# Four banks and a second pass for a fused layer's downsampling, with its constant operators made earlier

## The chip, the cores and the metric

The kernel runs on one core of one Trainium2 chip. The metric is the device time of one execution in microseconds; smaller is better. The program is written in Python on top of a planner: the program names the tiles, the instructions and the pools, and the planner places the instructions of each engine in an order of its own and adds the waits.

## The reference, cut to what matters

Four layers are computed on eight images of 512 channels by 32 x 32 pixels, in f32. Layer 0 is a group norm, a multi-head attention with an iterated tanh step, and a projection. Layer 1 is one attention over all 1024 pixels. Layer 3 is a bottleneck of mixed experts. The change concerns layer 2: every channel of every image is upsampled by two with a 12-tap filter, passed through a leaky ReLU, and downsampled by two with the same kind of filter.

```
out = input + bias
out = sep_upfirdn(out, up_filter * 2, up=2)
out = leaky_relu(out, 0.2) * sqrt(2)
out = sep_upfirdn(out, down_filter, down=2)
```

The filters are inputs, so the matrices that the kernel uses for them must be made on the chip.

## The kernel before, in words

An outer loop runs over the images. For each it does layer 0, layer 1 and layer 2, and stores the result; layer 3 follows for all images. The eight PSUM banks are in three pools: `ps_sc` has two tiles of two banks each, and `ps_tp` and `ps_mm` have two single banks each. SBUF tiles of the tag `tmp` (1024 columns) share six slots, those of the tag `half` (512 columns) two.

Layer 0 multiplies by blocks in Winograd's manner: `product` (L387 to L422) computes seven products named P1, C11, U2, U3, C22, C21 and C12 into three pairs of banks A, X and Y, and the callback `made` evicts each. For v the callback `positions` does it on VectorE (DVE). In the first image, the weights' sums are made on GpSimd (POOL) by `weight_sums`, one key after the other: q, k, v, inl, proj and v1. Each has a raw tile of tag `tmp` or of its own.

Layer 1 ends in `weighted_rows`, whose matmuls (L905) leave pixel rows in `y`. They are written to a padded image in DRAM and read back, with their halo, by `Halo.load`. In the first image `layer2_constants` follows. It builds the operators `up_op`, `up_left_op`, `dn_op`, `up63_op` and `dn63_op` in scratch columns of one `tmp` tile named `setup`: two loads of taps and ten iotas on POOL, then several hundred short instructions on DVE that compare an index with each tap's number and add.

Layer 2 has eight tiles of rows, t = 0 to 7. `upsample(t)` does four matmuls by column block c (each is two records in the trace), into banks that turn through `ps_sc` and `ps_tp`. The helper `leak` then makes the leaky ReLU in two steps, `leak` on ScalarE (ACT, L954) and `up` on DVE (L955). `downsample(first, last, ts_)` collects the rows of two or three tiles t. For each chunk of 128 channels, cc = 0 to 3, it opens a bank of `ps_mm` and adds one matmul per block (t, c) and per half of 64 channels (L995), then evicts the bank to `z`. The calls are

```
upsample 0 1 2   downsample(0, 13, (0, 1, 2))
upsample 3 4     downsample(9, 21, (3, 4))
upsample 5 6 7   downsample(17, 31, (5, 6, 7))
```

with a last small strip (`up_63`, L1031; `dn63_op`, L1003) before and in the third downsampling. The eviction is an ACT copy after the first call (L1009), two DVE instructions after the second (L1011, L1012), and a DVE addition, an ACT copy and a DVE reduction after the third.

The order of an engine's instructions is the planner's. It starts from its own times for each instruction and, among those that are ready, serves first what is written first. Exceptions are regions that the program marks with `tc.manual_schedule(engines=...)`, in which the named engines keep the written order among the region's instructions; layer 0's attention is one. SyncE's queue (SP) issues the loads of x, the weights and the halos; POOL's issues the taps and the stores of the weights' sums; ACT's issues most of the writes of `y`.

A second copy of the whole program with shifted exponents (`shifted`) follows in a conditional block. It runs only when sums overflow, which they do not with these inputs.

Of the kernel before, what the change touches and what calls it, by code (L numbers as in the profile page):

```python
# [12 lines left out]
ALU = mybir.AluOpType  # L13
AX = mybir.AxisListType
# [3 lines left out]
P = 128  # L18
B, C, H, W = 8, 512, 32, 32
S = H * W  # L20
CC = C // P
SC = S // P
HALF = 512
NH = 8
HD = C // NH
# [28 lines left out]
def tile_sequence(ctx: ExitStack, tc: tile.TileContext, a: dict, out: bass.AP, shifted: bool):  # L54
# [12 lines left out]
    def big_tile(name, shape):  # L67
        return big.tile(shape, F32, tag="big", name=name)

    def bank(pool=None, name="mm"):  # L70
        pool = pool or ps_mm
        return pool.tile([P, HALF], F32, tag="bank", name=name)

    def tmp(name, n=HALF):
        if n == HALF:
            return work.tile([P, n], F32, tag="half", name=name, bufs=2)
        return work.tile([P, n], F32, tag="tmp", name=name, bufs=6)
# [260 lines left out]
    def weight(key, b):  # L338
        if not b:
            return weight_sums(key, *weight_quarters(key, tmp(f"raw_{key}", S)))  # L340
        t = wpool.tile([P, len(PARTS), 2, QR], F32, tag="w", name=f"w_{key}_{b}", bufs=3)
        nc.sync.dma_start(t, stored[key])
        return t
# [225 lines left out]
    def layer0(b, x, norm, w):  # L569
# [9 lines left out]
        w["inl"] = weight("inl", b)  # L579
        all_of(product(f"k_{b}", w["k"], h, t, channels(f"k_{b}", k, qkv_b[:, CC : 2 * CC])))  # L580
        w["proj"] = weight("proj", b)
        early = small.tile([P, 1], F32, tag="early", bufs=1, name=f"early_{b}")
        tc.keep_in_program_order(nc.scalar.activation(early, eps, AF.Exp))
        all_of(product(f"v_{b}", w["v"], h, t, positions(f"v_{b}", v, v_row), rows=True))
# [19 lines left out]
        def scores(t):  # L604
            g, jc = divmod(t, SC)
            oc, sh = groups[g]
            pair = ps_sc.tile([P, S], F32, tag="scores", name=f"scores_{b}_{t}")
            ps = [pair[:, ts(r, HALF)] for r in range(2)]
            for r in range(2):
                for c in range(2):  # L610
                    nc.tensor.matmul(  # L611
                        ps[r][rows[c]],
                        k[rows[r], oc, jc * P + c * HD : jc * P + c * HD + HD],
                        q[rows[r], oc, ts(sh, HALF)],
                        start=True, stop=(shifts is None),
                    )
            if shifts is not None:
                for r in range(2):
                    nc.tensor.matmul(
                        ps[r], ones[HD * r : HD * r + 1, :],  # L620
                        shifts[HD * r : HD * r + 1, oc, ts(sh, HALF)],
                        start=False, stop=True, skip_group_check=True,
                    )
            e = tmp(f"e_{b}_{t}", S)
            nc.scalar.activation(e, pair, AF.Exp, scale=HD ** -0.5)  # L625
            exps[t] = e
            if jc == 1:
                accs[g] = sums(f"acc_{b}_{g}")
                nc.vector.tensor_add(accs[g], exps[t - 1], e)  # L629
            elif 1 < jc < SC - 1:  # L630
                nc.vector.tensor_add(accs[g], accs[g], e)  # L631
            elif jc == SC - 1:
                nc.vector.scalar_tensor_tensor(
                    accs[g], accs[g], 1.0, e, ALU.mult, ALU.add,
                    accum_out=seen_sums[:, b, g : g + 1],
                )
# [84 lines left out]
    def layer1(b, x, w, midway):  # L721
# [109 lines left out]
                midway()  # L831

        weighted_rows(b, eT, v, inv, y, written)
        if b == 0:
            layer2_constants()
        for t in range(3, NT):
            halo.load(t)
        halo.load_last()
# [108 lines left out]
    def layer2(b, halo, freed=lambda t: None):  # L947


        up = []  # L950

        def leak(dst, ps, name):
            t = tmp(f"leak_{name}")[0 : dst.shape[0], :]
            nc.scalar.mul(t, ps, 0.2 * SQRT2)  # L954
            nc.vector.scalar_tensor_tensor(dst, ps, SQRT2, t, ALU.mult, ALU.max)  # L955

        def upsample(t):
            if t % 2 == 0:
                two = big_tile(f"up_{b}_{t // 2}", [P, 8, C])
                up.extend(two[:, 4 * i : 4 * i + 4, :] for i in range(2))  # L960
            for c in (0, 2):

                n = 2 * t + c // 2
                if n % 3 == 2:
                    ps = [bank(ps_tp, name=f"up_{b}_{t}_{c + i}") for i in range(2)]
                else:
                    pair = ps_sc.tile([P, S], F32, tag="scores", name=f"up_{b}_{t}_{c}")
                    ps = [pair[:, ts(i, HALF)] for i in range(2)]
                for i in range(2):
                    _, n, op = halo.columns(c + i)  # L970
                    nc.tensor.matmul(  # L971
                        ps[i], op[0 : IR * n, :], halo.tile(t)[0 : IR * n, c + i, :],
                        start=True, stop=True,
                    )
                for i in range(2):
                    leak(up[t][:, c + i, :], ps[i], f"{b}_{t}_{c + i}")

        halves = [slice(0, HD), slice(HD, P)]  # L980

        def downsample(first, last, ts_):
            for cc in range(CC):
                zr = z[:, cc, :].rearrange("p (h w) -> p h w", w=W)
                ps = bank(name=f"dn_{b}_{cc}_{first}")
                rows = ps.rearrange("p (h w) -> p h w", w=W)
                blocks = [(t, c) for t in ts_ for c in range(4)]
                for i, (t, c) in enumerate(blocks):
                    r0, r1 = max(4 * t - 3, 0), min(4 * t + 5, H - 1)
                    c0, c1 = max(8 * c - 3, 0), min(8 * c + 10, W - 1)  # L990

                    k = P - UC if t == 0 else P
                    op = dn_op[0:k].rearrange("p (r c) -> p r c", c=OC)
                    for s, part in enumerate(halves):
                        nc.tensor.matmul(  # L995
                            rows[part, r0 - first : r1 + 1 - first, c0 : c1 + 1],
                            up[t][0:k, c, ts(2 * cc + s, HD)],
                            op[:, r0 - 4 * t + 3 : r1 + 4 - 4 * t, c0 - 8 * c + 3 : c1 + 4 - 8 * c],
                            start=(i == 0), stop=(last < H - 1 and i == len(blocks) - 1),
                            skip_group_check=True,  # L1000
                        )
                for s, part in enumerate(halves if last == H - 1 else ()):
                    nc.tensor.matmul(  # L1003
                        ps[part, (29 - first) * W : (32 - first) * W],
                        up63[:, ts(2 * cc + s, HD)], dn63_op,
                        start=False, stop=True, skip_group_check=True,
                    )
                if first == 0:
                    nc.scalar.copy(zr[:, 0:14, :], rows[:, 0:14, :])  # L1009
                elif first == 9:  # L1010
                    nc.vector.tensor_add(zr[:, 9:14, :], rows[:, 0:5, :], zr[:, 9:14, :])  # L1011
                    nc.vector.tensor_copy(zr[:, 14:22, :], rows[:, 5:13, :])  # L1012
                else:
                    nc.vector.tensor_add(zr[:, 17:22, :], rows[:, 0:5, :], zr[:, 17:22, :])
                    nc.scalar.copy(zr[:, 22:32, :], rows[:, 5:15, :])
                    nc.vector.tensor_reduce(pooled[:, cc, b : b + 1], z[:, cc, :], AX.X, ALU.add)
                    if b + 1 < B:
                        nc.sync.dma_start(spilled[b][ts(cc, P), :], z[:, cc, :])
            freed(ts_[-1])

        for t in range(3):
            upsample(t)
        z = big_tile(f"z_{b}", [P, CC, S])
        downsample(0, 13, (0, 1, 2))
        for t in (3, 4):
            upsample(t)
        downsample(9, 21, (3, 4))
        for t in (5, 6, 7):
            upsample(t)
        ps = bank(ps_tp, name=f"up_{b}_63")  # L1030
        nc.tensor.matmul(ps, up63_op[0 : 3 * W, :], halo.last, start=True, stop=True)  # L1031
        up63 = tmp(f"up63_{b}")
        leak(up63, ps, f"{b}_63")
        freed(6)
        downsample(17, 31, (5, 6, 7))
        return z

    with tc.tile_pool(name=f"weights_{run}", bufs=1) as wpool:
# [136 lines left out]
    def freed(t):  # L1175
        if t == 4:
            load_experts("w2_0", 3 * P)
            z3[0] = load_z(0)
        elif t == 6:
            for ky in (1, 2):  # L1180
                load_experts(f"w2_{ky}", 3 * P)
        elif t == 7:
            load_experts("w3", C)
# [119 lines left out]
```

## Time and profile before

| what | value |
|---|---|
| median of 3 runs | 3828.78 us (3828.47 to 3829.96) |
| the profiled execution | 3826.37 us, span 3824.6 us |
| TensorE (PE) busy | 3764.8 us, 98% |
| VectorE (DVE) busy | 2572.6 us, 67% |
| ScalarE (ACT) busy | 1202.9 us, 31% |
| GpSimd (POOL) busy | 100.3 us, 3% |
| dn matmuls, L995 | 4096 records, 210.5 us busy |
| up matmuls, L971 | 512 records in eight images |

In the profile, PE is the matmuls and PEld the weight loads that overlap them. Each f32 matmul is two records. A line of the timeline gives start, length, engine, line, operation, written and read tiles, shape and count, and in brackets the idle time of the engine ahead of it with what ended it.

### The profile page before, as it was taken

Reading aid. Unit: us, or ns where it says so; the run is one execution under the profiler, and the core shown is the slowest. Engines: PE = TensorE matmul, PEld = TensorE weight load, DVE = VectorE, ACT = ScalarE, POOL = GpSimd, SP = SyncE. Lnnn points to the kernel's source line nnn. Section 1 sums busy time; section 2 is a strip of 40 time slices with the busy share of each in tenths; the row PEclk is TensorE's granted clock in tenths of the full one; section 3 lists DMA queues with packets and bytes.
Section 4 is the critical chain, followed back from the end, with each engine's and each line's share of the span. In section 5 each row is a group of like instructions: output and inputs, shape, how many; then the busy total and the mean of one; then the engine's idle time right before and its main releaser. Section 6 shows DMA issues by size and latency. Waiting matters only on the chain.

```text
span 3824.6 us, 50438 instructions
## 1 busy us (share of the span) xinstructions
PE 3764.8 (98%) x20838; PEld 1996.0 (52%) x20838; DVE 2572.6 (67%) x3887; ACT 1202.9 (31%) x1707; POOL 100.3 (3%) x118
## 2 busy tenths in 40 slices
PE   8999999999999999999999999999999999999999
PEld 4346653475435753466534754357534754347543
DVE  5877948664686648775586647765487656866885
ACT  0631226212442116312252124422162123521333
POOL 5000000000000000000000000000000000001000
PEclk9999999999999999999999999999999999999999
DMA  5002310123101310023101220023201131003432
GB/s 199 24 1 86 115 63 1 42 76 106 39 1 61 121 70 11 1 85 119 58 1 61 84 92 27 1 80 102 80 1 42 52 129 41 1 1 124 161 145 98
DMA packets 85841, 248.67 MB, mean 65 GB/s; under 512 B 10480, under 2 KB 33024, under 8 KB 78816
## 3 DMA queue, kind: packets, MB, share of 16 engines
q1 hardware_dynamic: 69712, 220.23, 16.2%
q10 hardware_dynamic: 13824, 12.59, 1.0%
q0 software_dynamic: 2064, 12.51, 0.9%
q8 instruction: 166, 2.72, 0.3%
q14 instruction: 75, 0.61, 0.1%
HBM read 185.40 MB, written 59.90 MB: 64 GB/s over the span
## 4 chain that ended last, share of the span: by engine, by line
PE 93%; DVE 4%; ACT 1%; DMA 1%; issue 0%; SPq 0%; ACTq 0%; DVEq 0%
PE scores L611 12%; PE av L647 12%; PE inl_X L417 6%; PE dn L995 5%; PE v_X L417 4%; PE inl_A L417 4%; PE inl_Y L417 4%; PE up L971 4%; PE av_X L905 3%; PE c L1209 3%; PE v_Y L417 3%; PE av_A L905 3%; PE av_Y L905 2%; PE v_A L417 2%; PE proj_X L417 2%; PE q_X L417 2%
## 5 line engine op out<-in xcount | busy, mean ns | idle before, releaser
L625 ACT ACTIVATE e<-scores 128x1024 f32<-128x1024 f32 x512 | 523.2, 1024 | 673.5 <-PE scores L611 624.8
L611 PE MATMUL scores<-q,k 64*64 64x512 f32 x4096 | 535.8, 593 | 3.6 <-DVE v L498 3.6
L647 PE MATMUL av<-e,v 64*64 64x512 f32 x4096 | 531.0, 589 | 0.0
L631 DVE TENSOR_TENSOR acc<-acc,e 128x1024 f32<-128x1024 f32 x320 | 389.5, 1217 | 38.5 <-ACT e L625 36.5
L611 PEld LDWEIGHTS scores<-q,k 64*64 64x64 f32 x4096 | 153.8, 133 | 297.6 <-issue 208.5
L647 PEld LDWEIGHTS av<-e,v 64*64 64x64 f32 x4096 | 161.3, 133 | 278.2 <-issue 275.2
L417 PE MATMUL inl_X<-T_hf,w_inl 128*128 128x512 f32 x576 | 262.9, 592 | 0.0
L955 DVE SCALAR_TENSOR_TENSOR up<-up,leak 128x512 f32<-128x512 f32 x264 | 173.5, 688 | 115.3 <-ACT leak L954 110.0
L954 ACT ACTIVATE leak<-up 128x512 f32<-128x512 f32 x264 | 149.5, 596 | 249.5 <-DVE up L955 127.7
L668 DVE RECIPROCAL inv<-av 128x256 f32<-128x256 f32 x128 | 223.0, 1747 | 0.0
L995 PEld LDWEIGHTS dn<-dn_op,up 128*64 128x64 f32 (+1 forms) x4096 | 193.2, 136 | 56.5 <-issue 28.8
L995 PE MATMUL dn<-dn_op,up 128*64 128x126 f32 (+5 forms) x4096 | 210.5, 255 | 8.8 <-DVE up L955 7.9
L971 PE MATMUL up<-halo,up_op 126*128 126x512 f32 (+1 forms) x384 | 183.7, 611 | 0.8 <-DVE up L955 0.6
L417 PEld LDWEIGHTS inl_X<-T_hf,w_inl 128*128 128x128 f32 x576 | 108.7, 190 | 138.6 <-issue 105.8
L417 PE MATMUL inl_A<-hf,w_inl 128*128 128x512 f32 x384 | 172.2, 594 | 0.0
L511 ACT ACTIVATE inl_U<-inl_U,inl_b 128x512 f32<-128x512 f32 x96 | 66.7, 718 | 307.6 <-DVE inl_U L526 307.6
L629 DVE TENSOR_TENSOR acc<-e,e 128x1024 f32<-128x1024 f32 x64 | 78.8, 1232 | 112.0 <-ACT e L625 112.0
L522 DVE TENSOR_TENSOR inl_U<-inl_X,inl_P 128x512 f32<-128x512 f32 x96 | 61.9, 687 | 121.7 <-PE inl_X L417 118.9
L1209 PE MATMUL c<-rim,mixed 128*128 128x512 f32 x288 | 124.9, 592 | 0.0
L417 PEld LDWEIGHTS inl_A<-hf,w_inl 128*128 128x128 f32 x384 | 72.2, 190 | 94.6 <-issue 90.4
L905 PE MATMUL av_X<-v,eT 128*128 128x256 f32 x512 | 118.8, 380 | 1.8 <-DVE av_W L884 1.0
L905 PE MATMUL av_A<-v,eT 128*128 128x256 f32 x512 | 119.1, 381 | 0.0
(304 smaller groups left out, 5561.1 us busy)
## 6 DMA issues: line engine op xcount, KB each, us to landing
halo<-ypad_u SPq DMA_DIRECT2D x128, 252.0 KB
halo<-ypad_u SPq DMA_DIRECT2D x128, 198.0 KB
w_v<-stored_u_v SPq DMA_DIRECT2D x14, 1792.0 KB
x<-in_x_dram SPq DMA_DIRECT2D x32, 512.0 KB
spill_u<-z SPq DMA_DIRECT2D x28, 512.0 KB
z<-spill_u SPq DMA_DIRECT2D x28, 512.0 KB
out_dram<-z SPq DMA_DIRECT2D x28, 512.0 KB
w_q<-stored_u_q SPq DMA_DIRECT2D x7, 1792.0 KB
```

Of the source, the lines that this page charges most:

```text
L417: nc.tensor.matmul(dst, lhs, rhs, start=(opens and s == 0 and cc == 0), stop=(cc == 1 and s == rows), skip_group_check=True,)
L611: nc.tensor.matmul(ps[r][rows[c]], k[rows[r], oc, jc * P + c * HD : jc * P + c * HD + HD], q[rows[r], oc, ts(sh, HALF)], start=True, stop= ...
L625: nc.scalar.activation(e, pair, AF.Exp, scale=HD ** -0.5)
L631: nc.vector.tensor_add(accs[g], accs[g], e)
L647: nc.tensor.matmul(avs[g][r][rows[c]], v[rows[r], jc, ts(2 * oc + c, HD)], e[rows[r], ts(c, HALF)], start=(jc == 0), stop=(jc == SC - 1),)
L668: nc.vector.reciprocal(copies[g][:, at], totals[g][:, at])
L905: nc.tensor.matmul(ps[:, ts(s, QR)], left[:, j, at : at + P], right[:, j, :], start=(what in ("P1", "U2", "W") and s == 0 and j == 0), sto ...
L954: nc.scalar.mul(t, ps, 0.2 * SQRT2)
L955: nc.vector.scalar_tensor_tensor(dst, ps, SQRT2, t, ALU.mult, ALU.max)
L971: nc.tensor.matmul(ps[i], op[0 : IR * n, :], halo.tile(t)[0 : IR * n, c + i, :], start=True, stop=True,)
L995: nc.tensor.matmul(rows[part, r0 - first : r1 + 1 - first, c0 : c1 + 1], up[t][0:k, c, ts(2 * cc + s, HD)], op[:, r0 - 4 * t + 3 : r1 + 4 ...
L1209: nc.tensor.matmul(banks[g].rearrange("p (h w) -> p h w", w=W), wt[:, at : at + P], h1[:, ky + 16 * g : ky + 16 * g + 16, kx : kx + W], st ...
```

## The change

It has four parts. `layer2_constants()` is called in layer 0 of the first image, after the product for k and the request of the projection's weights, and no longer at the end of layer 1. The downsampling opens four banks at once, two of `ps_mm` and two of `ps_tp`; a first pass adds all rows of blocks but the last to each, and a second pass adds the last row and evicts. The upsampling's turn of banks is moved by one (`n % 3 == 1`). The PE instructions of layer 2 stand in a region of fixed order. Besides, a bias matmul of the shifted program is cut in two halves.

```
@@ layer0
         w["proj"] = weight("proj", b)
+        if b == 0:
+            layer2_constants()
         early = small.tile([P, 1], F32, tag="early", bufs=1, name=f"early_{b}")
...
@@ layer1
         weighted_rows(b, eT, v, inv, y, written)
-        if b == 0:
-            layer2_constants()
...
@@ layer2
-                if n % 3 == 2:
+                if n % 3 == 1:
                     ps = [bank(ps_tp, name=f"up_{b}_{t}_{c + i}") for i in range(2)]
...
+        def down_block(rows, cc, first, last, t, c, opens, closes):
...
         def downsample(first, last, ts_):
-            for cc in range(CC):
-                ps = bank(name=f"dn_{b}_{cc}_{first}")
-                blocks = [(t, c) for t in ts_ for c in range(4)]
-                for i, (t, c) in enumerate(blocks):
...
+            ends = last == H - 1
+            banks = [bank((ps_mm, ps_tp)[cc // 2], f"dn_{b}_{cc}_{first}") for cc in range(CC)]
+            for late in range(2):
+                for cc in range(CC):
+                    rows = banks[cc].rearrange("p (h w) -> p h w", w=W)
+                    for t in ts_[-1:] if late else ts_[:-1]:
+                        for c in range(4):
+                            down_block(
+                                rows, cc, first, last, t, c, t == ts_[0] and c == 0,
+                                late == 1 and c == 3 and not ends,
+                            )
+                    if late:
+                        evicted(cc, banks[cc], rows, first, ends)
             freed(ts_[-1])
...
+        with tc.manual_schedule(engines={mybir.EngineType.PE}):
+            for t in range(3):
+                upsample(t)
+            z = big_tile(f"z_{b}", [P, CC, S])
+            downsample(0, 13, (0, 1, 2))
...
```

`down_block` is the matmul pair of one block as before, and `evicted` the strip's matmuls and the eviction as before.

More of the change, by code (lines that the diff above doesn't have):

```diff
@@ L618, in scores @@
                 for r in range(2):
[L619 to L623, printed above, removed]
+                    for c in range(2):
+                        nc.tensor.matmul(
+                            ps[r][rows[c]], ones[HD * r : HD * r + 1, 0:HD],
+                            shifts[HD * r : HD * r + 1, oc, ts(sh, HALF)],
+                            start=False, stop=True,
+                        )
             e = tmp(f"e_{b}_{t}", S)
@@ L980, in layer2 @@
         halves = [slice(0, HD), slice(HD, P)]
-        def downsample(first, last, ts_):
-            for cc in range(CC):
-                zr = z[:, cc, :].rearrange("p (h w) -> p h w", w=W)
-                ps = bank(name=f"dn_{b}_{cc}_{first}")
-                rows = ps.rearrange("p (h w) -> p h w", w=W)
-                blocks = [(t, c) for t in ts_ for c in range(4)]
-                for i, (t, c) in enumerate(blocks):
[L989 to L1018, printed above, removed]
-            freed(ts_[-1])
@@ L1021, in layer2 @@
[L1021 to L1035, printed above, removed]
+        def down_block(rows, cc, first, last, t, c, opens, closes):
+            r0, r1 = max(4 * t - 3, 0), min(4 * t + 5, H - 1)
+            c0, c1 = max(8 * c - 3, 0), min(8 * c + 10, W - 1)
+            k = P - UC if t == 0 else P
+            op = dn_op[0:k].rearrange("p (r c) -> p r c", c=OC)
+            for s, part in enumerate(halves):
+                nc.tensor.matmul(
+                    rows[part, r0 - first : r1 + 1 - first, c0 : c1 + 1],
+                    up[t][0:k, c, ts(2 * cc + s, HD)],
+                    op[:, r0 - 4 * t + 3 : r1 + 4 - 4 * t, c0 - 8 * c + 3 : c1 + 4 - 8 * c],
+                    start=opens, stop=closes, skip_group_check=True,
+                )
@@ new lines, in downsample @@
+        def downsample(first, last, ts_):
+            ends = last == H - 1
[8 more added lines that the diff above has]
+                                late == 1 and c == 3 and not ends,
+                            )
+                    if late:
+                        evicted(cc, banks[cc], rows, first, ends)
+            freed(ts_[-1])
@@ new lines, in evicted @@
+        def evicted(cc, ps, rows, first, ends):
+            zr = z[:, cc, :].rearrange("p (h w) -> p h w", w=W)
+            for s, part in enumerate(halves if ends else ()):
+                nc.tensor.matmul(
+                    ps[part, (29 - first) * W : (32 - first) * W],
+                    up63[:, ts(2 * cc + s, HD)], dn63_op,
+                    start=False, stop=True, skip_group_check=True,
+                )
+            if first == 0:
+                nc.scalar.copy(zr[:, 0:14, :], rows[:, 0:14, :])
+            elif first == 9:
+                nc.vector.tensor_add(zr[:, 9:14, :], rows[:, 0:5, :], zr[:, 9:14, :])
+                nc.vector.tensor_copy(zr[:, 14:22, :], rows[:, 5:13, :])
+            else:
+                nc.vector.tensor_add(zr[:, 17:22, :], rows[:, 0:5, :], zr[:, 17:22, :])
+                nc.scalar.copy(zr[:, 22:32, :], rows[:, 5:15, :])
+                nc.vector.tensor_reduce(pooled[:, cc, b : b + 1], z[:, cc, :], AX.X, ALU.add)
+                if b + 1 < B:
+                    nc.sync.dma_start(spilled[b][ts(cc, P), :], z[:, cc, :])
@@ new lines, in layer2 @@
+        with tc.manual_schedule(engines={mybir.EngineType.PE}):
[3 more added lines that the diff above has]
+            downsample(0, 13, (0, 1, 2))
+            for t in (3, 4):
+                upsample(t)
+            downsample(9, 21, (3, 4))
+            for t in (5, 6, 7):
+                upsample(t)
+            ps = bank(ps_tp, name=f"up_{b}_63")
+            nc.tensor.matmul(ps, up63_op[0 : 3 * W, :], halo.last, start=True, stop=True)
+            up63 = tmp(f"up63_{b}")
+            leak(up63, ps, f"{b}_63")
+            freed(6)
+            downsample(17, 31, (5, 6, 7))
```

## The prediction

> **What bounds the kernel now.** I read the page's busy times first, then TensorE's timeline around layer 2 of every image, then the table of stages, then the operators' own instructions.
>
> ```profile
> PE 3764.8 (98%) x20838; PEld 1996.0 (52%) x20838; DVE 2572.6 (67%) x3887; ACT 1202.9 (31%) x1707; POOL 100.3 (3%) x118
> ```
>
> PE is busy for 98% of the span, so only two things can shorten it: its gaps, and stretches in which it is busy at a lower clock. The change adds or removes no executed matmul. PE's timeline in layer 2 of the first image, then of the third:
>
> ```profile
> 410.49 2.74 PE L971 MATMUL up<-halo,up_op 126*128 126x512 f32 x6
> 419.69 0.59 PE L301 MATMUL gn_var<-gdev,group_mean 128*128 128x4 f32 x2 [6.47 <-DVE gdev L299]
> 420.14 2.05 PE L971 MATMUL up<-halo,up_left_op 99*128 99x512 f32 x2
> 421.99 4.89 PE L971 MATMUL up<-halo,up_op 126*128 126x512 f32 x6
> ...
> 430.24 8.88 PE L995 MATMUL dn<-dn_op,up 112*64 112x66 f32 x192
> ...
> 1307.37 0.46 PE L995 MATMUL dn<-dn_op,up 112*64 112x66 f32 x8
> ...
> 1313.11 9.13 PE L995 MATMUL dn<-dn_op,up 112*64 112x84 f32 x184
> ...
> 1329.24 3.79 PE L995 MATMUL dn<-dn_op,up 128*64 128x99 f32 x64
> 1332.95 1.13 PE L971 MATMUL up<-halo,up_left_op 99*128 99x512 f32 x2
> 1334.01 3.31 PE L995 MATMUL dn<-dn_op,up 128*64 128x99 f32 x64
> ```
>
> The reader is to see a 6.47 us gap in the first image, after which six upsampling records take 4.89 us instead of 2.74. The third image has no such gap. A table of two stages gives the price. Each runs from the same group of matmuls, the second av_Y group of layer 1's product C12, to the last L1003 group of layer 2:
>
> ```profile
> 1286.84:1358.99 72.15, 71.48 (x666) 49.52 (x665) 44.15 (x83) 23.66 (x42) 0.00 (x0) 1.00 0.44 146
> 392.72:475.88 83.16, 74.48 (x663) 50.28 (x663) 73.96 (x363) 23.56 (x42) 0.00 (x0) 0.94 0.39 127
> ```
>
> Columns: stage, length, busy us of PE, PEld, DVE, ACT, POOL, granted clock, DMA share, GB/s. The same PE work takes 83.16 us in the first image and 72.15 in the third, with 73.96 us of DVE work instead of 44.15. The extra DVE work is the operators (tile setup):
>
> ```profile
> 384.00:409.50 25.50, 17.40 (x173) 0.00 (x0) 1.00 0.44 138
> 409.50:422.50 13.00, 11.28 (x109) 0.00 (x0) 0.75 0.64 201
> 422.50:442.00 19.50, 11.39 (x80) 0.00 (x0) 0.90 0.51 159
> ```
>
> DVE only: 40.1 us in 362 instructions. From 409.5 to 422.5 they fill DVE and go ahead of gdev and of the leaks (L955), which PE waits for.
>
> **What the Trainium skill says.** "TensorE: Matmul & The Clock Gate", in "What's actually happening", puts the idle window after which the clock halves at about 3.4 us. The trace agrees: after 6.47 us, records go from 0.43 to 0.86 us apart for about 7 us. [...] "SBUF — State Buffer", in "Terms", says that DVE and GpSimd share a port pair and the loser blocks. Here four acc additions (L631) take 6.99 us from 99.1 on, while POOL forms w_v; their mean over the run is 1.22 us.
>
> **The change, part by part.**
>
> *Operators moved from layer 1's end to between the first image's k and v.* The whole 83.16 - 72.15 = **11.0 us** of excess should go: the gap, the slow clock behind it, and three gaps of 0.95, 0.88 and 0.38 us behind av_X groups, which other images fill with early upsampling matmuls. In the first image those could not start early, since up_left_op is finished only at 409.4. Late next is what the third image has, the leaks, already in its 72.15. Ends: -8 to -12.
>
> *What the move costs where it lands.* Every instruction goes along: 362 on DVE, two loads of taps (0.58 and 0.54 us of issue) and ten iotas (1.10 us) on POOL; none on SP or ACT. POOL has room before w_proj's sums (13.26 us idle before 69.64). If the loads stand behind w_inl's sums, which end at 55.4, the operators start near 58; if before them, near 51. A slot of tag tmp (six) is free once q's temporaries are, about 46.9. DVE's room:
>
> ```profile
> 47.00:71.00 24.00, 24.00 (x61) 11.20 (x60) 6.80 (x10) 4.03 (x6) 6.95 (x7) 1.00 0.44 159
> 71.00:94.00 23.00, 23.00 (x110) 19.78 (x112) 9.36 (x15) 0.00 (x0) 5.92 (x6) 1.00 0.33 125
> ```
>
> 17.2 + 13.6 = 30.8 us idle for 40 us of work, so about 9 us run on into the attention. Worse, in the old place the operators went ahead of every instruction written after them: gmean waited from 391.9 to 418.6, and leaks flow only from 422.5, when 28.7 us of them (17.40 + 11.28) are done. The rest is mostly a serial chain (L180, L181), which lets others between. In the new place v's evictions come after them. From 51 to 71 DVE has 20 - 6.8 = 13.2 us for operators, so some 15 us still stand ahead of v_P (71.3 now): it comes near 86. PE has v's first product (to 72.9) and two independent ones (U2 and C22, 3.45 us each), so it runs dry at about 80. A wait of 6 us and about 3.5 us of half clock behind it make 9.5. The planner that orders the engines may mix better (2 us), or POOL's later place may make it 18 (wait of 13, clock 3.5, a slower start of the attention, which has one e slot fewer). I take **+8**; ends +1 and +18. Layer 2 had 28.7 us of the same work ahead of its leaks and lost 11, so this is of the right size.
>
> *Four banks, last row of blocks in a second pass.* Same blocks, same instructions. Before, chunk 0 needs the newest row of leaks after a third (rows 0-2) or half (3, 4) of its blocks; now 128 or 64 instructions stand in front, 5.9 or 3.0 us at 46 ns each (8.88/192). A leak is there about 2 us after its matmul (0.6 on ACT, 0.69 on DVE, signals), so this wait goes. Price: .46 + 9.13 - 8.88 = 0.7 us in the first stage, 3.79 - 3.31 = 0.5 in the second. *PE's order fixed*: three cuts of each image go (dn x8 among the ups, the second stage's split, q_X before the last two chunks). A cut costs about 0.22 us (the up pair after it takes 1.12 instead of 1.02, and 0.12 at dn's end): 0.7. Together 1.9. What comes new: the up pair numbered 10 takes banks of ps_tp just after chunks 2 and 3 of rows 3-4, whose eviction on DVE (0.32 + 0.415 us) must end, with further leaks queued behind those evictions on DVE; PE waits 0.2 to 0.6 us. And ps_tp evictions are bunched in the second pass: ACT's four copies of 0.53 us fit its 0.77 us per chunk. Net -1.2 per image in seven images: **-8.4**; ends +3 and -13. The last image, whose waits are its own, I leave out.
>
> *The last image's gap* (5.62 us at 3524.26, then half clock) comes from eight mixed instructions (L1150) that stand ahead of the leaks on DVE. DVE's order is not fixed by the change: **0**, but it may be dealt anew, -8 to +5.
>
> *The upsampling's bank turn* (n % 3 == 1) keeps three pairs in use: 0. *The bias matmuls in two halves* are in the shifted program, which isn't run: 0.
>
> **Sum:** -11.0 + 8 - 8.4 + 0 = -11.4. The profiled execution took 3826.4 us (span 3824.6), 2.4 below the median of 3828.8. So 3815.0 for a profile like it, and 3817.4 against the median. A measurement of this kernel can tell about 0.2%, 7.7 us, from no change.
>
> **Rivals.**
> 1. *Slower.* The tap loads stand on POOL behind w_proj's sums, which end at 76.2. The operators then start near 80 and 28.7 us of them go ahead of v's later evictions and of acc, in a stage where DVE has little room (about 9 of 10 us busy from 110 on). PE waits some 27 us, less 5 of independent work, with 3.5 of half clock and a slow start of the attention: about +33. With -11 and -8.4 that is +13: 3842. It decides from a wait of 27 us on. For it: POOL serves the sums in the order written. Against: POOL waits 13 us there, and the old taps were issued as soon as POOL was free. 0.12.
> 2. *No change.* The wait moves from layer 2 to v one for one (+11 to +18), and the second pass only exchanges waits (-2): -11 + 11 - 2, so 3827. Or "order fixed" holds all other matmuls out of layer 2, so that the av_X gaps that upsampling fills now (0.95 + 0.88 + 0.38 us in the first image) open in six images: +13, which with the sum's -11.4 makes 3830. 0.28.
> 3. *More than forecast.* v's evictions pass between the operators (+1) and the last image's gap goes (-8): -26, so 3802. 0.12, within faster.
>
> **How the numbers follow.** The forecast with its own scatter holds 0.48, and with rival 3 faster has 0.60; within 0.2% 0.28; slower 0.12. The range goes from rival 3's value to rival 2's worse half and part of rival 1: 3802 to 3837.
>
> **What would show it.** In the new profile: setup instructions from about 50 to 105 us; a PE gap with v_P as its end near 80 to 86 and slow v records behind it; no gap at gn_var in the first image, and av_X groups with up records between them; the first image's stage near 72 us; dn groups of 192 and 128 in one piece with no wait on L955. Wrong it would be if v showed no gap (then faster), if up records stood behind all of av_X, or if up pair 10 waited over 1 us for z.

## The result and the profile after

The changed kernel takes **3820.1 us** (median of 14 runs, 3817.3 to 3822.0) against 3828.8 us (3826.0 to 3831.3): a ratio of 0.9976, interval 0.9970 to 0.9983. Its profiled execution has a span of 3818.3 us, 6.3 less than the profiled execution before. The predicted 3817.4 us is close, but two of its terms were far off, in opposite directions.

The page after: TensorE's busy time, then its two groups of layer 2 (line, engine, operation, count; busy us and mean ns; idle time ahead of it).

```profile
PE 3747.4 (98%) x20838; PEld 1992.0 (52%) x20838; DVE 2582.9 (68%) x3887; ACT 1202.2 (31%) x1707; POOL 98.6 (3%) x118
...
L990 PE MATMUL dn<-dn_op,up 128*64 128x99 f32 (+5 forms) x4096 | 194.0, 253 | 0.0
L972 PE MATMUL up<-halo,up_op 126*128 126x512 f32 (+1 forms) x384 | 182.0, 602 | 8.7 <-DVE up L956 8.7
```

PE is busy for 17.4 us less with the same 20838 records. 16.5 of them are the dn matmuls (210.5 before). Their idle time of 8.8 us is not all saved: the up records now have 8.7 (0.8 before), and 6.97 of that is the last image's gap. The span fell by only 6.3. Where the rest went is in v of the first image. PE's timeline of v in the kernel before, and then in the changed kernel:

```profile
69.38 7.07 PE L417 MATMUL v_A<-w_v,h 128*128 128x256 f32 x32
...
81.47 3.62 PE L417 MATMUL v_X<-w_v,T_h 128*128 128x256 f32 x16
84.92 1.89 PE L417 MATMUL v_Y<-w_v,T_h 128*128 128x256 f32 x8
86.64 3.62 PE L417 MATMUL v_X<-w_v,T_h 128*128 128x256 f32 x16
```

```profile
76.16 3.62 PE L417 MATMUL v_Y<-w_v,T_h 128*128 128x256 f32 x16
96.35 6.36 PE L417 MATMUL v_A<-w_v,h 128*128 128x256 f32 x16 [16.57 <-DVE setup L180]
102.55 3.62 PE L417 MATMUL v_X<-w_v,T_h 128*128 128x256 f32 x16
107.97 3.69 PE L417 MATMUL v_X<-w_v,T_h 128*128 128x256 f32 x16 [1.80 <-DVE setup L180]
...
118.83 3.60 PE L613 MATMUL scores<-q,k 64*64 64x512 f32 x16 [2.71 <-DVE setup L160]
```

Before, v has no gap. Now there is one of 16.57 us, then sixteen records that take 6.36 us where their like take 3.62 (the first twelve come 0.43 us apart instead of 0.22), then two gaps more. The profile puts each gap down to an operator on DVE, though that is not the whole cause of the second (below). The table of stretches says what DVE did in the changed kernel (length, busy us of PE, PEld, DVE, ACT, POOL, clock, DMA share, GB/s), and the same for the tile setup alone (DVE and POOL columns only):

```profile
80.00:96.40 16.40, 0.05 (x1) 0.05 (x1) 16.40 (x154) 0.00 (x0) 0.00 (x0) 0.64 0.13 53
96.40:115.00 18.60, 16.80 (x64) 13.77 (x64) 17.31 (x94) 0.00 (x0) 0.00 (x0) 0.86 0.00 1
```

```profile
47.00:60.00 13.00, 0.00 (x0) 2.18 (x12) 1.00 0.71 248
62.00:94.70 32.70, 28.71 (x254) 0.00 (x0) 0.85 0.24 89
```

The taps and iotas are on POOL from 56.24 to 58.4, behind w_inl's sums. DVE, idle for most of the time before 60, does its first operator at 62.09, and 28.71 us of them stand ahead of v_P (now at 94.73, before at 71.31).

PE's timeline in layer 2 of the first image, where the kernel before has the gap of 6.47 us:

```profile
428.74 0.28 PE L301 MATMUL gn_var<-gdev,group_mean 128*128 128x4 f32 x2
428.88 1.10 PE L972 MATMUL up<-halo,up_op 126*128 126x512 f32 x2
429.82 3.62 PE L906 MATMUL av_X<-v,eT 128*128 128x256 f32 x16
...
442.45 8.51 PE L990 MATMUL dn<-dn_op,up 112*64 112x66 f32 x192
...
457.96 6.41 PE L990 MATMUL dn<-dn_op,up 128*64 128x99 f32 x128
```

There is no such gap, upsampling stands between the av_X groups, and the dn groups of 192 and 128 are in one piece. The two stages of the prediction's table (83.16 and 72.15 us before) are now

```profile
417.19:485.23 68.04, 67.79 (x664) 48.57 (x663) 42.26 (x81) 23.05 (x41) 0.00 (x0) 1.00 0.43 136
1294.62:1363.82 69.20, 67.95 (x664) 48.71 (x663) 42.14 (x81) 23.16 (x41) 0.00 (x0) 1.00 0.41 134
```

(two q_X records, 1.06 us, have left the third image's stage). How far the changed kernel is behind or ahead of the kernel before, read at the same group of matmuls in both timelines: +25.3 at the end of the first image's attention, +10.3 at the second image's attention, then +7.8, +5.8, +3.1, +0.1, -2.6, -5.8 at the next ones, -6.7 at layer 3, -6.2 at its end. So v costs 25.4 us, the first image's layer 2 gives 15, the six middle images 16.1, the last 0.9.

### The profile page after: what moved, and what is told of

It is laid out like the page before. It is cut to its first block, busy times and chain, and to the rows that moved or that the text cites. A ratio compares the mean times of both kernels' runs of the same rounds, so it can differ in the third digit from the quotient of the medians.

```text
span 3818.3 us, 50444 instructions
## 1 busy us (share of the span) xinstructions
PE 3747.4 (98%) x20838; PEld 1992.0 (52%) x20838; DVE 2582.9 (68%) x3887; ACT 1202.2 (31%) x1707; POOL 98.6 (3%) x118
## 4 chain that ended last, share of the span: by engine, by line
PE 94%; DVE 3%; ACT 1%; DMA 1%; issue 0%; SPq 0%; ACTq 0%; DVEq 0%
PE scores L613 12%; PE av L650 12%; PE inl_X L417 6%; PE up L972 5%; PE dn L990 5%; PE inl_A L417 4%; PE inl_Y L417 4%; PE v_X L417 4%; PE av_X L906 4%; PE c L1222 3%; PE av_A L906 3%; PE v_Y L417 3%; PE av_Y L906 3%; PE v_A L417 2%; PE proj_X L417 2%; PE q_X L417 2%
## 5 line engine op out<-in xcount | busy, mean ns | idle before, releaser
L990 PE MATMUL dn<-dn_op,up 128*64 128x99 f32 (+5 forms) x4096 | 194.0, 253 | 0.0
L972 PEld LDWEIGHTS up<-halo,up_op 126*128 126x128 f32 (+1 forms) x384 | 72.3, 192 | 97.7 <-issue 68.3
```

The costliest lines, as they stand in the source:

```text
L972: nc.tensor.matmul(ps[i], op[0 : IR * n, :], halo.tile(t)[0 : IR * n, c + i, :], start=True, stop=True,)
L990: nc.tensor.matmul(rows[part, r0 - first : r1 + 1 - first, c0 : c1 + 1], up[t][0:k, c, ts(2 * cc + s, HD)], op[:, r0 - 4 * t + 3 : r1 + 4 ...
```

## The experiments

Each was timed beside the kernel before. The first two set the theory that the move costs more in v (25.4 us) than it gains in layer 2 (about 12) against the rival that the move is what gained. The prediction had the move gain 3 us. The next three take banks, pass and order apart, and the rest look for a better place and order of service for the operators.

**1. Operators back at layer 1's end**, the rest of the change kept.

```
@@ layer0 / layer1
-        if b == 0: layer2_constants()      (between k and v)
+        if b == 0: layer2_constants()      (layer 1's end)
```

> The changed kernel with layer2_constants() back at the end of layer 1; banks, second pass and fixed order stay. Theory (the move costs 25.4 us in the first image's v and saves about 12 in its layer 2): 3820.1 - 25.4 + 12 = 3807, a gap of 6 to 7 us and slow records again in the first image's layer 2, no gap in v. Rival (the move is what gained, the banks did little): 3826 to 3829.

Measured: 3810.3 us (ratio 0.9954, 0.9940 to 0.9967), 9.8 *less* than the changed kernel (8.4 by the ratios), near the first theory and far from the rival. PE's timeline of this run has the gap again, and longer:

```profile
419.94 0.59 PE L301 MATMUL gn_var<-gdev,group_mean 128*128 128x4 f32 x2 [8.19 <-DVE gdev L299]
```

**2. Only the move**, in the kernel before.

```
@@ layer0, between k and v
+        if b == 0: layer2_constants()
@@ layer1, end
-        if b == 0: layer2_constants()
```

> The kernel before with only the move of layer2_constants() to behind k. Theory: the gap of 16.6 us in v comes as in the changed kernel, +25.4, and the first image's layer 2 is 12 shorter: 3828.8 + 25.4 - 12 = 3842, slower. Rival (the move gains): 3817 to 3822.

Measured: 3841.5 us (1.0031, 1.0018 to 1.0043), 12.7 more than before, as expected. v loses 27.1 us, the first image's layer 2 gains 12.5, nothing else moves. PE's timeline in v:

```profile
97.88 6.59 PE L417 MATMUL v_A<-w_v,h 128*128 128x256 f32 x16 [16.32 <-DVE setup L180]
```

Both runs say the same: the move is a **loss** of about 8 to 13 us, and the change is faster in spite of it.

**3. Experiment 1 without the region of fixed order.**

```
-        with tc.manual_schedule(engines={mybir.EngineType.PE}):
```

> As e1_ops_back, but without the region of fixed order: four banks, second pass, upsampling's bank turn. If banks and second pass save the 2.7 us per image: 3807 to 3809, like e1. If the fixed order saves part of it (the planner cuts dn again with up and q records, 0.22 us each, three cuts): 3811 to 3814. If the order does all: 3826.

Measured: 3806.4 us (0.9945, 0.9932 to 0.9959), 3.8 less than experiment 1. PE's timeline shows the third image's first two stages of dn, which took 9.13 (with 0.46 ahead) and 3.79 + 3.31 before:

```profile
1303.45 0.45 PE L990 MATMUL dn<-dn_op,up 112*64 112x66 f32 x8
...
1309.18 8.28 PE L990 MATMUL dn<-dn_op,up 112*64 112x84 f32 x184
...
1324.46 6.41 PE L990 MATMUL dn<-dn_op,up 128*64 128x99 f32 x128
```

Banks and second pass keep the gain without any fixed order; one of the three cuts (dn x8) comes back, and it is not slower for it.

**4. Only the fixed order**, in the kernel before (two banks, one pass).

```
+        with tc.manual_schedule(engines={mybir.EngineType.PE}):
```

> The kernel before with PE's order fixed in layer 2, two banks and one pass. Theory (banks and pass do the saving; without fillers the dn waits for leaks and for a bank's eviction stand open): 3829 to 3835. Rival (the order alone saves the cuts, 0.7 us in seven images): 3823 to 3825.

Measured: 3847.7 us (1.0048, 1.0034 to 1.0062), 18.6 more (13 to 24 by the interval). The first theory had the sign, but neither had a loss of this size. PE's timeline of the third image shows what the planner's freedom had covered:

```profile
1322.34 6.62 PE L995 MATMUL dn<-dn_op,up 128*64 128x99 f32 x148 [0.38 <-DVE up L955]
...
1338.97 5.03 PE L995 MATMUL dn<-dn_op,up 128*64 128x99 f32 x100 [0.92 <-DVE up L955]
```

dn waits for leaks with nothing allowed ahead of it. What I had priced as "cuts" were matmuls that the planner put into such waits.

**5. Four banks, one pass** (experiment 3 with each chunk filled in one go), to tell banks and pass apart.

```
-            for late in range(2):
-                for cc in range(CC):
-                    for t in ts_[-1:] if late else ts_[:-1]:
+            for cc in range(CC):
+                for t in ts_:
```

> Operators at layer 1's end, planner's order, four banks opened at once, but each chunk's bank is filled in one pass (all rows of blocks, then evicted, as in the kernel before). If the second pass is what saves the waits for the newest leaks (2.0 us of the 2.9 per image), most of the 22.7 us gain of banks and pass together is lost: 3820 to 3826. If four banks alone give it, by freeing the eviction from the next chunk's path, it stays near 3806.

Measured: 3819.4 us (0.9978, 0.9969 to 0.9986). By the ratios the four banks are worth 0.22% and the pass, against experiment 3, another 0.33%. (The upsampling's moved turn of banks goes with the four banks here; no run has it alone.) The profile agrees on the pass: in PE's timeline of the third image the first dn stage is as long as before, and the second keeps its wait,

```profile
1312.36 9.15 PE L990 MATMUL dn<-dn_op,up 112*64 112x84 f32 x184
...
1328.51 6.95 PE L990 MATMUL dn<-dn_op,up 128*64 128x99 f32 x128
```

and within the first of these groups there are two pauses of 0.36 and 0.40 us between one record and the next, where experiment 3 has none over 0.12. Per middle image the banks give 1.3 us and the pass 1.6 (shifts between timelines). In this image the banks' part comes from the second stage, no longer split around an up pair, and from the third, with no q_X inside.

**6. Operators served last.** The changed kernel, with the planner told to place the operators behind all other ready work.

```
+            tc.cur_priority += LATER
             layer2_constants()
+            tc.cur_priority -= LATER
```

> The changed kernel with its operators emitted at the same place, between k and v, but with the planner told to serve them last of all that is ready, so that they only fill DVE's idle time. The number of instructions is unchanged. If the 25 us that the first image's v loses are a matter of order (about 29 us of operators stand ahead of v_P on DVE), they go: the v stage within 1 us of the kernel before, and 3820 - 25.4 + 1 = about 3796. The rival, that the 40 us of added DVE work are themselves too much for the stages they land in (the attention's acc additions then come late), leaves 3812 to 3820.

Measured: 3811.3 us (0.9956, 0.9942 to 0.9969): 8.8 less than the changed kernel, not 24. My theory was half right. v is nearly whole (PE's largest waits in it are 1.92 and 0.73 us, the attention begins 3.5 us later than before), but the attention then loses 13 more. PE's timeline there, and DVE's time on the operators alone (length, DVE, POOL, clock, DMA share, GB/s):

```profile
117.87 1.27 PE L618 MATMUL scores<-q,k 64*64 64x512 f32 x8 [1.99 <-ACT e L633]
...
128.31 1.97 PE L668 MATMUL av<-acc,ones 128*64 128x512 f32 x4 [7.46 <-DVE setup L167]
```

```profile
97.00:129.00 32.00, 22.61 (x155) 0.00 (x0) 0.84 0.19 75
```

From 97 to 129 the operators hold DVE for 22.61 of 32 us. The acc additions, 1.7 us apart before, come 3.9 us apart with some fifteen chained operators between two of them. Part of the delay is not order: beside POOL's sums of w_v three operators took 1.2 us each, and the first acc addition came at 105.89 instead of 97.39 (3.5 us of that are the later start). For the rest this reading fits: "last" is last in the planner's own time, and an engine's order is then fixed, so where the chain runs slower than the planner thought, everything behind it waits. The planner's own times are not on record, so this is not shown.

**7. The same without the fixed order in layer 2.**

```
-        with tc.manual_schedule(engines={mybir.EngineType.PE}):
```

> The kernel with operators served last, and in addition without the region that fixes PE's order in layer 2. If the fixed order costs what it cost with the operators at their old place (3820 - 3810 against 3806: 3.8 us), this is 3.8 below the run with the region, about 3792 to 3794. The rival, that the fixed order only costs where the operators stand at layer 1's end, leaves both equal within 2 us.

Measured: 3808.9 us (0.9950, 0.9937 to 0.9964). Missed by 15 us as the run before was; the difference to that run, 2.4 us, has the sign of experiments 1 and 3. Each of the two differences lies inside the intervals. So with four banks the fixed order costs little: 2 to 4 us by the medians, none to 3.6 by the spans of the profiles, which is not clear of the noise.

**8. The last image's mixing dealt**: of the eight instructions that stood ahead of its leaks, the one on ACT is issued after row tile 3, and the seven on DVE one or two at a time after row tiles 3 to 7.

```
+            upsample(t)
+            dealt(t)
```

> The same without the region, and in the last image eight of the mixed experts' instructions (one ACT, seven DVE of w1 for the first image) are placed one or two at a time behind the leaks of row tiles 3 to 7, instead of all ahead of the leaks. If these eight are the cause of the last image's gap (6.97 us of PE, and about 3 of half clock behind it), it goes: 8 us less than without, about 3785. The rival, that the leaks behind them are delayed in turn by the same work, leaves the time the same within 2 us.

Measured: 3803.1 us (0.9933, 0.9920 to 0.9947), 5.8 less. The last image itself gains about 8 us, as expected. Some 2 us were lost again in the first image, which the edit does not touch: in its v, one wait of 1.96 us is followed by slow records (5.55 us for sixteen), where run 7 has two waits of 0.90 and 0.59 us and no slow record. The last image's gap in PE's timeline, in run 7 and then in this one:

```profile
3509.31 0.71 PE L995 MATMUL dn<-dn_op,up 112*64 112x66 f32 x8 [5.61 <-DVE up L961]
```

```profile
3505.70 1.99 PE L977 MATMUL up<-halo,up_op 126*128 126x512 f32 x4 [0.50 <-DVE up L961]
```

**9. Operators at layer 1's start, served last**, on top of run 8.

```
@@ layer0, between k and v
-            (the operators)
@@ layer1, start
+        if b == 0:
+            tc.cur_priority += LATER
+            layer2_constants()
+            tc.cur_priority -= LATER
```

> The best kernel so far (no fixed order, last image's mixing dealt), with its operators emitted at the start of layer 1 of the first image and served last of all that is ready, not between k and v. DVE is idle there for 47 of the 120 us from 230 to 350 us, against 31 of 47 us before v's end and 5 to 7 in each 40 us of attention. If the cost of the move is DVE's room in the attention (8 us of waits before the first acc-ones product), it goes, and layer 2's gain of about 12 us stays: 3803 - 18.7 + (0 to 5) = 3785 to 3790. The rival, that the planner puts the serial chain ahead of layer 1's evictions as it did with the attention's acc additions, loses it again: 3798 to 3806.

Measured: 3795.7 us (0.9912, 0.9897 to 0.9927). Between the two theories: v and the attention are free (+1.6 us against the kernel before at the first inl product, where run 8 has +19.1), layer 2 gains about 15, but layer 1 loses 8.7. PE waits behind operators there too, only less, as its timeline shows:

```profile
350.13 2.07 PE L274 MATMUL scores<-qk 64*128 64x512 f32 x2 [2.37 <-DVE setup L183]
352.13 5.74 PE L420 MATMUL v_X<-w_v,T_x 128*128 128x256 f32 x16
```

**10. The same place, served in the order written.**

```
-            tc.cur_priority += LATER
             layer2_constants()
-            tc.cur_priority -= LATER
```

> The same place, but served in the order written, ahead of layer 1's own work on DVE. By the theory that order of service is one part of the cost and room the other, this is above the run that serves them last: some of the 29 us of parallel instructions stand ahead of the sums and evictions of qk and v1, a PE wait of 5 to 15 us, 3793 to 3803. The rival, that room alone decides, leaves both equal within 3 us.

Measured: 3805.0 us (0.9937, 0.9923 to 0.9951), 9.3 more than run 9, a little above what was expected. PE waits 7.62 us at once behind setup in v1, with slow clock after it. So order of service decides here too, and room alone does not.

**11. In front of the first inl product, served last**: 29 us of idle DVE in a stage that has most of them in one piece.

```
@@ layer0, after the attention (and no longer in layer1)
+        if b == 0:
+            (the operators, as in run 9)
         for it in range(3):
```

> The kernel with operators at layer 1's start, served last, with one thing changed: they are emitted in front of layer 0's first inl product of the first image, directly behind the attention, so that they are spread over 210 to 320 us (29 us of idle DVE between 210 and 310) and nothing of them is left for layer 1's scores and totals, where that kernel still loses about 8.5 us (waits of 0.30, 0.88, 0.85 and 2.37 us and slow records behind them). If the rest of the cost is there, 3796 - 8.5 + (0 to 3) = 3787 to 3790. The rival, that the inl stage's evictions are delayed instead, gives 3794 to 3800.

Measured: **3791.8 us** (0.9905, 0.9888 to 0.9921), 37.9 less than before and the best of all; the edits of runs 7 and 8 are in it. The table of stretches for the operators alone, DVE column first:

```profile
205.00:230.00 25.00, 5.25 (x69) 2.18 (x12) 1.00 0.02 1
230.00:265.00 35.00, 16.44 (x150) 0.00 (x0) 1.00 0.00 1
265.00:300.00 35.00, 10.26 (x87) 0.00 (x0) 1.00 0.15 56
300.00:330.00 30.00, 8.56 (x60) 0.00 (x0) 1.00 0.33 128
```

It is the same work, 40.5 us, spread over 116 us (213.3 to 328.9), with the clock at 1.00 all along. One wait of 2.46 us is left at the start: inl_X waits for T_hf, with operators ahead of it on DVE. From the first inl product to the first of layer 1 this run loses 4.8 us. The expectation of 3787 to 3790 was just missed.

## Why the prediction was right, and where it was wrong

- **-11.0 for layer 2 without the operators: right, a little small.** The move alone gains 12.5 there. The signs named for it were found: no gap at gn_var, up records between av_X groups.
- **+8 for v: the term that failed, and by three times.** It was 25.4, outside its own end of 18: 16.57 + 1.80 + 2.71 of gaps and 4.4 of slow clock, less the 0.45 that was there, make 25.0. Wrong was first of all the room that the operators were set against, DVE's idle time from 51 to 71 (13.2 us). They began at 62.09, since the taps came behind w_inl's sums and DVE had k's eviction first, so v_P came at 94.7 and not 86. That later start was in the text as the end of 18, with a wait of 13.
- **Why even that end was short.** The 28.7 us ahead of v_P came to the digit (28.71), but by luck. They are 254 instructions, where 282 went ahead in the old place, and four of them, which ran beside POOL's sums of w_proj, took 4.97 us, 4.2 more than their like in the old place. The prediction names such a case for acc, and has nothing for it in this sum. It also has nothing for the two evictions v_P and v_P_hi that free the bank (1.6 us from the start of the first), nor for the two later gaps. The last gap is behind what is left of the operators, which the prediction said lets others between: v_Y ends at 115.1 and its eviction begins at 117.1. The gap of 1.80 us is for the most part v_X's own eviction, two v_U of 0.68 us each. In the kernel before, eight v_Y records cover that eviction; here all sixteen stand ahead of the long wait.
- **Rival 1's mechanism, without its cause.** The wait was of its size (27 - 5 predicted, 21 in three gaps), although the taps were not behind w_proj's sums. Its +33 also has about 7.5 for a slow start of the attention; that start lost 3.9. Rival 2's "one for one" was closer on the move than the forecast, and still too kind: it is a net loss of about 8 to 13 us. Its other form, that the fixed order keeps the ups from between the av_X groups, did not come: in the third image two pairs stand there, as before.
- **-1.2 per image for banks, pass and order: right in mechanism, half in size.** The six middle images give 2.0 to 3.2 each, 2.7 in the mean. The dn stages of the third image lost 1.04, 0.69 and 0.49 us, against 0.7 and 0.5 priced, with nothing for the third stage. The new wait of up pair 10 (0.2 to 0.6) is 0.03 us: evictions of chunks 2 and 3 are done in time. A wait of 0.22 us did appear elsewhere, at the up pair before the first dn stage. First image included (2.4 of its 14.9), this term is about -18.5 instead of -8.4. What differs between the middle images is PE's gaps alone. Without the gaps each of the six saves 2.6 us; the rest, -0.6 to +0.6, is for the most part waits for the halo's DMA and for leaks, which differ from image to image in both kernels.
- **Fixed order as a gain of 0.7 per image: wrong in sign.** It costs 18.6 us in the kernel before, and a few at most with four banks. A cut of 0.22 us is what the planner pays to fill a wait. That the second pass takes those waits away is the likely reason why the order does little harm here, though no run has the fixed order with four banks and one pass. It is not why the change is faster.
- **Last image 0: right** (-0.9). Its gap is 6.97 us now. Run 7, without the fixed order, still has 5.61 of it, and dealing the eight instructions out takes it away.

So the total held by luck: an error of +17.4 in v met errors of about -12.5 in layer 2. Still open is what the upsampling's turn of banks does by itself.

## What to carry to other kernels

When setup work is moved to where an engine is idle, count the idle time between the moment its inputs are there and the first deadline behind it, and the order in which that engine serves them; here the same 40 us cost 25 us between k and v, some 12 at layer 1's end and, served last, about 5 before the inl product. In a reduction over tiles whose newest part is late, hold all accumulators open and add the newest part last. Before fixing an engine's order by hand, look at what the free order had put into the waits.

## What the runs showed of the hardware

The clock can halve without one long gap. In the first image's q of run 9, two waits of 2.26 and 1.68 us with 1.10 us of matmuls between them were followed by slow records, where in the kernel before 1.32 and 1.69 us were not (six records in 2.84 us). PE's timeline of run 9, and then of the kernel before:

```profile
26.17 1.10 PE L420 MATMUL q_X<-T_h,w_q 128*128 128x512 f32 x2 [2.26 <-DVE T_h L385]
28.95 4.34 PE L420 MATMUL q_X<-T_h,w_q 128*128 128x512 f32 x6 [1.68 <-DVE T_h L385]
```

```profile
28.85 2.84 PE L417 MATMUL q_X<-T_h,w_q 128*128 128x512 f32 x6 [1.69 <-DVE T_h L382]
```

Its attention is 1.6 us late from there on. In v of the first image a single wait made the difference, and hardly by its length. In run 8, records 0.43 us apart instead of 0.22 begin five records after a wait of 1.96 us; in run 6, at the same place, none do after 1.92 us. PE's timeline of run 8, and then of run 6:

```profile
75.74 5.55 PE L420 MATMUL v_A<-w_v,h 128*128 128x256 f32 x16 [1.96 <-DVE v_P_hi L487]
```

```profile
74.54 1.99 PE L420 MATMUL v_A<-w_v,h 128*128 128x256 f32 x8 [1.92 <-DVE v_P_hi L487]
```

The Trainium skill, "TensorE: Matmul & The Clock Gate", section "What's actually happening", describes a window of activity that runs freely and does not restart with the kernel. These cases fit that, though so few do not prove it. Each of these waits is shorter than the 3.4 us that the prediction names, so an idle stretch of that length was not needed here.

Short DVE instructions can be long beside POOL. While POOL forms w_v from 115.20 on in the changed kernel, two additions of one column to the setup tile took 1.38 us together, by DVE's timeline,

```profile
115.16 1.38 DVE L164 TENSOR_TENSOR setup<-setup 128x1 f32<-128x1 f32 x2
```

where the pair ahead of it took 0.35. Ahead of v_P one such addition lasts just as long as the sum of w_proj beside it, by the timelines of DVE and of POOL:

```profile
72.44 1.24 DVE L181 TENSOR_TENSOR setup<-setup 128x1 f32<-128x1 f32 x1
```

```profile
72.40 1.27 POOL L363 TENSOR_TENSOR w_proj<-w_proj 128x512 f32<-128x512 f32 x1 [0.17 <-DMA w_proj<-in_proj_wT_dram]
```

"SBUF — State Buffer", section "Who interferes with whom", says that a DVE instruction with two SBUF inputs contends with a GpSimd one that reads SBUF. The additions agree; three of the long ones are TENSOR_SCALAR and not additions. The operators took 48.2 us of DVE in the new place and 40.1 in the old. Nine instructions account for the difference: they ran beside POOL's sums of w_proj and w_v for 0.5 to 1.3 us each, 8.6 us more than their like in the old place. In run 11, where POOL forms no sums beside them, the operators take 40.5.
